# Attention beside a depthwise convolution: key blocks in batches of 7, 7, 7, 7 and 8, and other places for the small steps

## The chip, the cores and the metric

The kernel runs on one core of one Trainium2 chip. The metric is device time in microseconds (us) of one execution. The engines are TensorE (PE, its weight loads PEld), VectorE (DVE), ScalarE (ACT), GpSimd (POOL) and SyncE (SP); SP and POOL are used here mostly to issue DMA transfers.

## What is computed

```python
B, C, H, W = 4, 384, 48, 48          # N = 2304 tokens, 8 heads of 48
x_flat = x.reshape(B, C, N).transpose(0, 2, 1)
local = depthwise_conv_7x7(x) * bn_scale + bn_shift
local_q = layernorm(local_flat)                      # over channels
q, k, v = heads(layernorm(x_flat) @ qkv_w.T + qkv_b)
q = q + heads(local_q)
attn = softmax(q @ k.T * 48 ** -0.5)
out = x_flat + (attn @ v) @ proj_w.T + proj_b        # back to B, C, H, W
```

Everything is fp32.

## The kernel before

**Tiling.** Channels lie on the 128 partitions (three chunks), tokens along the free dimension. An image has NA = 5 groups of image rows for its queries (ROWS = 8, 10, 10, 10, 10, so 384 or 480 columns), 20 groups t = 5b + g in all. Keys and values are made per image in six parts of 384 tokens. Eight heads make four pairs; a pair's 2304 keys are 18 blocks of 128, so a group has 4 x 18 = 72 blocks.

**Order of the stages.** The first image's keys and values are made (0 to 152 us), then the loop over t at L1314 runs. Ahead of each later image's first group stands a key and value stage (L1316 to L1383), in which the output projection of the image before runs too. Then comes the loop over slots (L1389 to L1489), in which the group's attention runs.

**A slot.** A group has NSLOT = 12 slots, each a batch of BATCH = 6 blocks. `score_batch` (L1156) scores six blocks: `score` (L1126) is six matmuls (three passes, as queries and keys are split into a high and a low part of type fp32r, times two halves of the rows, one head each; L1133), and then ScalarE's exponential of the block (L1141) into a `pt` tile. `weigh_batch` (L1163) weighs them: `weigh` (L1144) is two fp32 matmuls of the 128 weights by the values and a column of ones (L1148; the trace shows four records a block), summed over the batch in one PSUM tile "o". `sums_out` copies the sums out on ScalarE: those of a pair's first batch into `ao` (or `aot` for the last pair, L1035), the others into a `part_o` tile (L1025), which VectorE adds later (`sums_add`, L1044). Scores and sums share the PSUM pool: four buffers of two banks, handed out in turn. There are four `pt` buffers and two of `part_o`.

**Keys.** A pair's high and low keys lie in DRAM (`wide`) and come in thirds of six blocks, 768 KB each, into one of three `ks` buffers (`load_keys`, L788, DMA at L791), most of them requested on POOL two slots ahead.

**Query parts.** `high_queries` (L992) writes the high part of a pair's queries on ScalarE (L996); `low_queries` (L998) the low part on VectorE (L1001), and sends both to other partitions by small DMAs on SP. The next pair's are made in the first slot of each pair: high after scoring, low after weighing. The last pair's queries are first gathered from the ends of the other three, by eight DMAs on SP (`gather_tails`, L721, into the tile `qt`). The last pair's outputs are sent back by six DMAs on SP at the end of `sums_add`.

**What runs beside it.** VectorE makes the next group's convolution, 49 taps for each of three chunks (`conv_ops`, L334; one instruction of L365 each, and the first tap on ScalarE by `first_taps`), from a slab of x that `load_slab` (L129) requests on POOL when the convolution of the group before begins. After it come the layer norm of the result (`Norm`, L567): a sum over chunks, a sum over partitions through DRAM (`out`, L661), `few_centre`, squares on ScalarE, again a sum, `few_root`, and its addition to the queries (`query_end`, L972). Groups t to 3 use a variant with means on TensorE (`early`). The next image's x is loaded in parts (`load_x`, L124) and normed in the same way. The output of the group before is divided by its denominators (`divide`, L1063) and held in DRAM (`hold`, L1096).

**Who sets the order.** The orders of TensorE, VectorE, ScalarE and SP are those in which the program is written; only POOL's is left to the framework's scheduler. A planner (`spare` L458, `plan` L528, `convolve` L542) deals the convolution's taps out over two points a slot, by guesses of VectorE's free time at each (`spare`) and by the point at which each group's convolution is due.

The functions that the change touches, and their callers:

Of the kernel before, what the change touches and what calls it, by code (L numbers as in the profile page):

```python
# [25 lines left out]
BATCH = 6  # L26
NSLOT = 12
X_SLOTS = 4, 7
X_LATER = 3
OUT_SLOT = 7  # L30
WARM = 14
SHIFTS = 4
AHEAD = 18
FIRST_ROOM = 4.0
# [14 lines left out]
def unshifted_pass(  # L49
# [119 lines left out]
    third = BATCH * P  # L169
# [164 lines left out]
    def conv_ops(t):  # L334
        b, g = divmod(t, NA)
        if 0 < t < NT - 1:
            load_slab(*divmod(t + 1, NA))
# [11 lines left out]
        for i, (tap, c) in enumerate(order):  # L349
            if i == len(order) - AHEAD and t + 1 < NT:  # L350
                if t:
                    begin_sums(t + 1)
                soon.append(lambda: first_taps(t + 1))
            part = window(slab, acc[:, c, :], g, first, end, c, tap)
            if not part:
                continue
            src, dst = part
            weight = cw[:, c, tap : tap + 1]
            if tap == taps[0]:
                if t == 0:  # L360
                    nc.vector.tensor_scalar(
                        dst, src, weight, shift[:, c : c + 1], ALU.mult, ALU.add
                    )
            else:
                nc.vector.scalar_tensor_tensor(dst, src, weight, dst, ALU.mult, ALU.add)  # L365
            if t == 0 or tap != taps[0]:
                yield
# [85 lines left out]
    def norm_slots(t):  # L453
        return (8 - (t > 0), None) if t + 1 < NA else (5, 8)

    def spare(t, s, half):
        b, g = divmod(t, NA)
        first, second = norm_slots(t)  # L458
        time = 3.6 - (0.0 if half else 0.6) - (0.6 if half and s % 3 == 1 else 0.0)
        if b + 1 < B and g >= begins(b + 1):  # L460
# [5 lines left out]
        if t + 1 < NA:  # L466
            if t:
                time -= {
                    (first, 0): 1.3,
                    (first + 1, 0): 1.4,  # L470
                    (first + 1, 1): 1.3,
                    (first + 2, 1): 4.3,
                    (first + 3, 1): 0.6,
                }.get((s, half), 0.0)
            else:
                time -= {(first + 1, 0): 1.4, (first + 2, 0): 4.3, (first + 2, 1): 0.6}.get(
                    (s, half), 0.0
                )
        elif g < NA - 1:
            time -= {  # L480
                (3, 1): 2.3, (5, 0): 1.2, (5, 1): 2.2, (6, 1): 2.3, (8, 0): 0.4, (8, 1): 1.5,
                (9, 0): 4.5,
            }.get((s, half), 0.0)
        return max(0.3, time) * columns_of(t) / G
# [21 lines left out]
    for t in range(NT):  # L506
# [3 lines left out]
        points += [("slot", t, s, h) for s in range(NSLOT) for h in range(2)]  # L510
        room += [spare(t, s, h) for s in range(NSLOT) for h in range(2)]
# [4 lines left out]
    for t in range(1, NT):  # L516
        last = ("slot", t - 1, norm_slots(t - 1)[0] - (t >= NA), t < NA) if t % NA else ("kv", t, 4, 0)
# [203 lines left out]
    def gather_tails(dst, src):  # L721

        for i, c in enumerate((*range(CC), 0)):
            for r in (0, 64):
                nc.sync.dma_start(
# [67 lines left out]
    def from_x(b, g, before=None, ao=None):  # L793
# [22 lines left out]
        def key(u, r):  # L816
# [7 lines left out]
            else:  # L824
                k = work.tile([P, 2, GM], HALF, tag="pt", name=f"k{b}_{g}_{u}", bufs=4)[:, :, :G]
# [146 lines left out]
    def query_end(t, at_once=False):  # L972
# [3 lines left out]
        q3 = work.tile([P, GM], F32, tag="qt", name=f"qt{t}", bufs=1)[:, : columns_of(t)]  # L976
        queries[t] = q, q3
# [36 lines left out]
    ended = []  # L1014
    parts_of = deque()

    def sums_out():

        if not ended:
            return  # L1020
        t, p, i, sums = ended.pop()
        n = columns_of(t)
        if i:
            part = work.tile([P, GM], F32, tag="part_o", name=f"o{t}_{p}_{i}")[:, :n]
            nc.scalar.copy(part[0 : 64 + HA], sums[0 : 64 + HA, 0, :n])  # L1025
            parts_of.append((t, p, i, part))
            return
        if p == 0:
            ao = work.tile([P, CC, GM], F32, tag="ao", name=f"ao{t}")[:, :, :n]
            ao3 = work.tile([P, GM], F32, tag="aot", name=f"aot{t}", bufs=1)[:, :n]  # L1030
            den = dram.tile([NH, n], F32, tag=f"den{n}", name=f"den{t}")
            outputs[t] = ao, ao3, den
        ao, ao3, den = outputs[t]
        dst = ao[:, p, :] if p < CC else ao3
        nc.scalar.copy(dst[0 : 64 + HA], sums[0 : 64 + HA, 0, :n])  # L1035

    def sums_add():
# [3 lines left out]
        t, p, i, part = parts_of.popleft()  # L1041
        ao, ao3, den = outputs[t]
        dst = (ao[:, p, :] if p < CC else ao3)[0 : 64 + HA]
        nc.vector.tensor_add(dst, dst, part[0 : 64 + HA])  # L1044
        if i < KB // BATCH - 1:
# [4 lines left out]
        if p == NP - 1:  # L1050
            for c in range(CC):
                for r in (0, 64):
                    nc.sync.dma_start(
# [69 lines left out]
    jobs, between = deque(), deque()  # L1123
    weighing = deque()

    def score(t, p, kb):  # L1126
        ks, qs = stacks[t // NA, p, kb // BATCH], stacked[t, p]
        at = slice(kb % BATCH * P, (kb % BATCH + 1) * P)
# [11 lines left out]
        pt = work.tile([P, 2, GM], F32, tag="pt", name="pt", bufs=4)[:, :, :n]  # L1140
# [3 lines left out]
    def weigh(i, sums):  # L1144
        t, p, kb, pt = weighing.popleft()
        for j in range(2):
            first = (kb % NB * NH + 2 * p + j) * HA
            nc.tensor.matmul(  # L1148
                sums[halves[j], 0, : columns_of(t)],
                lhsT=values[t // NA, kb // NB][:, first : first + 64],  # L1150
                rhs=pt[:, j, :],
                start=i == 0,
                stop=i == BATCH - 1,
            )

    def score_batch(t, s):  # L1156
        p, k0 = s // (KB // BATCH), s % (KB // BATCH) * BATCH
        for kb in range(k0, k0 + BATCH):
            score(t, p, kb)
            if between:  # L1160
                between.popleft()()

    def weigh_batch(t, s):  # L1163
        p, i = s // (KB // BATCH), s % (KB // BATCH)
# [4 lines left out]
        sums = two_banks("o")  # L1169
        for n in range(BATCH):  # L1170
            weigh(n, sums)
        ended.append((t, p, i, sums))
        sums_out()
# [139 lines left out]

    for t in range(NT):  # L1314
        b, g = divmod(t, NA)
        if g == 0 and b:  # L1316

            sums_add()
            load_x(b, NG - 1)
# [68 lines left out]
        first, second = norm_slots(t)  # L1388
        for s in range(NSLOT):  # L1389
            pair, part = divmod(s, KB // BATCH)  # L1390
            score_batch(t, s)
            if part == 0 and pair < NP - 1:
                high_queries(t, pair + 1)
            if s == 0:
                gather_tails(*reversed(queries[t]))
            if s == 0 and g == 0:
                keep_stack(b, 2)
            if (s or g) and (s < NSLOT - 2 or g < NA - 1):
                load_keys(b, s + 2, nc.scalar if g == 0 and s < 3 else nc.gpsimd)
            if s == 2 and g:  # L1400
                rb = divide(t - 1)
            if s == 0 and coming:
                load_x(b + 1, g - begins(b + 1))
            if s == NSLOT - 4 and g == NA - 1:
# [4 lines left out]
                else:  # L1409
                    places = [("acc", 3)] * 3 + [("sq", 2)] * 2 + [("qs", 5)]  # L1410
                    aos = []
                    for i in range(NG):
                        load_residual(b, i, *places[i])
                        aos.append(fetch(b, i) if i < NG - 1 else outputs[t][0])
            if coming and s == X_SLOTS[1] + 1:
                norm_x.scale(norm_x.few_newton())
            if following and s == second + 1:
                local_end(t + 1, norm.few_newton())
                query_end(t + 1, True)
            if coming and s == X_SLOTS[0] + 1:  # L1420
                jobs.extend(norm_x.square_jobs())
            if following and s == first + 1:
                jobs.extend(norm.square_jobs())
            if coming and s == X_SLOTS[1]:
                norm_x.few_variance()
            if following and s == second:
                norm.few_variance()
# [3 lines left out]
            else:  # L1431
                convolve("slot", t, s, 0)
            sums_add()
# [8 lines left out]
            if coming and s == X_SLOTS[1]:  # L1442
                norm_x.few_root()
            if following and s == second:
                norm.few_root()
# [3 lines left out]
            weigh_batch(t, s)  # L1449
            if early and s == first:  # L1450
# [5 lines left out]
            if early and s == first + (2 if t == 0 else 3):  # L1456
                low_queries(t + 1, 0, nc.gpsimd if t == 0 else nc.sync)
            convolve("slot", t, s, 1)
            if t and early and s == first + 2:
                local_end(t + 1, norm.newton())  # L1460
                query_end(t + 1)
            if part == 0 and pair < NP - 1:
                low_queries(t, pair + 1)
            if t and early and s == first + 1:
                norm.sum_squares()
            if following and s == second + 1:
                low_queries(t + 1, 0)
            if coming and s == X_SLOTS[0]:
                norm_x.few_centre()
            if following and s == first:  # L1470
                norm.few_centre()
            if s == OUT_SLOT and g:
                ao = outputs[t - 1][0]
                nc.vector.tensor_mul(ao, ao, rb)
                hold(t - 1)
            if coming and s == X_SLOTS[0] - 2:
                norm_x = Norm(xn[b + 1, g - begins(b + 1)])
                norm_x.sum()
                norm_x.out()
            if coming and s == X_SLOTS[0] + 1:  # L1480
                norm_x.sum_squares()
                norm_x.out()
# [566 lines left out]
```

## Time and profile before

| | |
|---|---|
| time, median of 4 runs | 2728.52 us (2726.93 to 2730.58) |
| the profiled execution | 2728.94 us, of which the span 2726.9 us |
| instructions | 46025 |
| attention of a ten-row group | 108.9 us |
| attention of an eight-row group | 88.5 us |
| key and value stage of images 1 to 3 | about 140 us each |
| the end (last projection and output) | 35 us |

The span runs from the first to the last instruction that the profile shows. TensorE's records carry modelled ends, since matmuls are pipelined: two that run in two halves of the array at once are booked at once, and a slower step between two matmuls is booked as busy. Register, branch, semaphore and DMA-issuing instructions count as no busy time, except that GpSimd's DMA issues are shown under POOL. The granted clock of TensorE is 1.0 in all stages but the last (0.99).

### The profile page before, as it was taken

To read this page: it belongs to the slowest core of one execution; us is meant where nothing else is said; L and a number is where in the kernel's file an instruction comes from. 1 tells how busy PE (TensorE), PEld (TensorE's weight loads), DVE (VectorE), ACT (ScalarE), POOL (GpSimd) and SP (SyncE) were. 2 spreads that over 40 slices of the span, in tenths; PEclk is the share of its full clock that TensorE was granted. 3 is DMA by queue.
4 is the path that set the end of the run, shared out by engine and by line. 5 is a ranking of instruction groups with operands and counts; after the bars stand their busy time and mean duration, and the time that the engine had idled before them with its cause. 6 is when DMAs were issued, how large, how long until landed. Compare 5 with 4: busy or idle time off the path is not lost.

```text
span 2726.9 us, 46025 instructions
## 1 busy us (share of the span) xinstructions
PE 2712.0 (99%) x16448; PEld 1533.2 (56%) x16448; DVE 2315.9 (85%) x4042; ACT 1671.2 (61%) x2318; POOL 591.1 (22%) x1055
## 2 busy tenths in 40 slices
PE   9999999999999999999999999999999999999999
PEld 6555555555556655555555655555555665555555
DVE  8999999989899999989889999889888888986212
ACT  4367767777325767676622777767752377776762
POOL 3531111102452111011155211111225501110110
PEclk9999999999999999999999999999999999999999
DMA  8454544546455545455455553545635544444442
GB/s 175 90 147 134 140 117 128 128 139 163 126 146 156 137 129 130 126 141 134 135 147 134 163 148 115 144 123 138 158 102 159 152 138 130 140 132 133 138 150 68
DMA packets 160209, 370.46 MB, mean 136 GB/s; under 512 B 58273, under 2 KB 107394, under 8 KB 159970
## 3 DMA queue, kind: packets, MB, share of 16 engines
q0 software_dynamic: 70496, 277.44, 35.4%
q1 hardware_dynamic: 84016, 79.92, 12.9%
q10 hardware_dynamic: 5458, 10.06, 1.2%
q8 instruction: 132, 2.16, 0.3%
q14 instruction: 107, 0.88, 0.1%
HBM read 258.14 MB, written 64.14 MB: 118 GB/s over the span
## 4 chain that ended last, share of the span: by engine, by line
PE 90%; DVE 5%; DMA 3%; ACT 0%; issue 0%; SPq 0%; POOL 0%; DVEq 0%; POOLq 0%; ACTq 0%
PE o L1148 41%; PE r L1133 34%; PE r L719 16%; DVE acc L365 4%; DMA xn<-in_x_dram 1%; DMA qs<-qs 0%; DMA staged<-in_qkv_wT_dram 0%; DVE k L829 0%; DMA slab<-in_x_dram 0%; DMA four<-parts 0%; PE r L618 0%; DMA wide<-k 0%; DMA out_dram<-xr 0%; DVE xn L714 0%; DMA parts<-part 0%
## 5 line engine op out<-in xcount | busy, mean ns | idle before, releaser
L365 DVE SCALAR_TENSOR_TENSOR acc<-slab,vec,acc 128x470 f32<-128x470 f32 (+10 forms) x2832 | 1657.7, 657 | 2.0 <-ACT acc L328 2.0
L1141 ACT ACTIVATE pt<-r 128x960 f32<-128x960 f32 (+1 forms) x1440 | 1248.5, 942 | 248.4 <-PE o L1148 153.0
L1148 PE MATMUL o<-pt,v 128*64 128x480 f32 (+1 forms) x5760 | 1166.2, 554 | 0.4 <-ACT pt L1141 0.4
L1133 PE MATMUL r<-qs,ks 64*128 64x480 f32 (+1 forms) x8640 | 966.8, 373 | 5.1 <-DMA qs<-qs 3.1
L1133 PEld LDWEIGHTS r<-qs,ks 64*128 64x128 f32 x8640 | 783.7, 184 | 269.7 <-issue 172.2
L1148 PEld LDWEIGHTS o<-pt,v 128*64 128x64 f32 x5760 | 392.5, 137 | 659.9 <-issue 566.2
L791 POOL DMA_DIRECT2D ks<-wide x220 | 160.1, 728 | 1362.8 <-PE r L1133 1285.6
L719 PE MATMUL r<-xn,w_qk 128*128 128x384 f32 x864 | 284.2, 486 | 0.0
L1025 ACT COPY o<-o 113x480 f32<-113x480 f32 (+1 forms) x160 | 87.1, 544 | 277.0 <-PE o L1148 276.4
L719 PEld LDWEIGHTS r<-xn,w_qk 128*128 128x128 f32 x864 | 164.0, 190 | 114.7 <-issue 0.7
L719 PE MATMUL r<-w_v,xn 128*128 128x384 f32 x432 | 145.3, 489 | 1.8 <-DVE xn L714 1.2
L813 ACT COPY v<-r 128x384 f32<-128x384 f32 x72 | 32.1, 480 | 185.0 <-PE r L719 185.0
L1044 DVE TENSOR_TENSOR ao<-ao,o 113x480 f32<-113x480 f32 (+1 forms) x120 | 75.9, 632 | 73.6 <-ACT o L1025 73.6
L719 PEld LDWEIGHTS r<-w_v,xn 128*128 128x128 f32 x432 | 81.2, 190 | 61.7 <-DVE xn L714 3.6
L776 POOL DMA_DIRECT2D wide<-k x144 | 72.3, 503 | 99.7 <-ACT k L826 79.4
L1001 DVE TENSOR_TENSOR qs<-xn,qs 128x480 fp32r<-128x480 f32 (+1 forms) x60 | 37.9, 632 | 62.1 <-ACT qs L996 62.1
L719 PE MATMUL r<-af,w_o 128*128 128x384 f32 (+1 forms) x270 | 85.2, 470 | 0.0
L1035 ACT COPY ao<-o 113x480 f32<-113x480 f32 (+1 forms) x60 | 32.7, 544 | 72.0 <-PE o L1148 72.0
L1044 DVE TENSOR_TENSOR aot<-aot,o 113x480 f32<-113x480 f32 (+1 forms) x40 | 25.3, 632 | 56.9 <-ACT o L1025 56.9
L843 ACT ACTIVATE xn<-r,qkb 128x384 f32<-128x384 f32 x72 | 39.7, 577 | 52.1 <-PE r L719 48.6
L1114 DVE SCALAR_TENSOR_TENSOR xr<-r,pb,xr 128x384 f32<-128x384 f32 (+2 forms) x72 | 42.0, 611 | 33.8 <-PE r L719 26.0
L719 PEld LDWEIGHTS r<-af,w_o 128*128 128x128 f32 x270 | 51.3, 190 | 31.9
(154 smaller groups left out, 1339.7 us busy)
## 6 DMA issues: line engine op xcount, KB each, us to landing
ks<-wide POOLq DMA_DIRECT2D x220, 768.0 KB, 4.9
qs<-qs SPq DMA_DIRECT2D x349, 60.0 KB
slab<-in_x_dram POOLq DMA_DIRECT2D x22, 432.0 KB, 7.9
wide<-k POOLq DMA_DIRECT2D x96, 96.0 KB, 2.2
wide<-ks POOLq DMA_DIRECT2D x12, 768.0 KB, 5.6
xr<-in_x_dram POOLq DMA_DIRECT2D x16, 576.0 KB, 5.3
rb<-rden SPq DMA_DIRECT2D x32, 270.0 KB
held<-ao POOLq DMA_DIRECT2D x12, 720.0 KB, 3.8
```

The lines of the kernel that those rows point to most:

```text
L365: nc.vector.scalar_tensor_tensor(dst, src, weight, dst, ALU.mult, ALU.add)
L719: nc.tensor.matmul(dst, lhsT=weights(c), rhs=src(c), start=c == 0, stop=c == CC - 1)
L776: nc.gpsimd.dma_start(out=last[16 * u : 16 * u + 16, 0], in_=k[r : r + 16, 0])
L791: queue.dma_start(out=place_keys(b, p, i), in_=wide[b, p][:, :, at])
L843: nc.scalar.activation(src[:, i, :], q[:, :G], AF.Identity, bias=qkb[:, 0, i : i + 1])
L1001: nc.vector.tensor_sub(qs[:, 1, :], query_of(t, p), qs[:, 0, :])
L1025: nc.scalar.copy(part[0 : 64 + HA], sums[0 : 64 + HA, 0, :n])
L1044: nc.vector.tensor_add(dst, dst, part[0 : 64 + HA])
L1114: nc.vector.scalar_tensor_tensor(xr[:, co, :], m, pb[:, co : co + 1], xr[:, co, :], ALU.add, ALU.add)
L1133: nc.tensor.matmul(r[:, j, :n], lhsT=ks[rows, w, at], rhs=qs[rows, m, :], start=i == 0, stop=i == 2,)
L1141: nc.scalar.activation(pt, r[:, :, :n], AF.Exp, scale=SCALE)
L1148: nc.tensor.matmul(sums[halves[j], 0, : columns_of(t)], lhsT=values[t // NA, kb // NB][:, first : first + 64], rhs=pt[:, j, :], start=i == ...
```

## The change

- **Batches.** Groups t from 4 on (`few_slots`, 16 of 20) have 10 slots with batches of 7, 7, 7, 7, 8, 7, 7, 7, 7 and 8 blocks; groups 0 to 3 keep 12 of 6. Batches 2 and 7 hold the end of one pair and the start of the next: `weigh_batch` makes two sums for them. `sums_out` and `sums_add` know first and last sums instead of batch numbers, and in those two slots `sums_add` is called once more.
- **Buffers.** `pt` has five buffers instead of four, `part_o` one instead of two; the last pair's output takes the `qt` tile, that of the gathered queries, instead of one of its own.
- **Keys.** Third i+3 is requested in the slot in which third i's last block is scored.
- **Queries.** High and low parts of the next pair are made in slots 0, 2 and 5 (of 12) or 0, 2 and 4 (of 10) instead of 0, 3 and 6. The high part of the next group's first pair is made behind the fifth score of slot 7, its low part at that slot's end; before, they were made in slots 9 (of 12).
- **Tails.** `gather_tails` and the six DMAs of the last pair's output go to POOL, in slot 1 or 2 (the latter ones stay on SP ahead of a key and value stage and at the end).
- **Places.** Two tables say in which slot and at which of its four points each norm step, the division, the multiplication and the loads stand. The steps of a 10-slot group lie in other slots than those of a 12-slot group.
- **Loads.** The next slab is requested after 40 taps of a convolution rather than at its start; the next image's x during the group before the one in which it is normed, in slot 6 or 8, rather than in slot 0 of that group.
- **Planner.** `spare` has new guesses for 10 slots, and the convolution is due one slot after `q_sum`, slot 3 of 10.

The core of the diff (left out: the guesses in `spare`, the closures that call each step where its table says, and the lines that they replace):

```diff
-BATCH = 6
-NSLOT = 12
+THIRD = 6
+PLACES_10 = {
+    "x_sum": (1, 3), "x_centre": (3, 1), "x_squares": (3, 1), "x_sum_squares": (3, 3),
+    "x_variance": (5, 1), "x_root": (5, 1), "x_scale": (5, 3),
+    "next_x": (6, 0), "divide": (1, 1), "tails": (1, 3), "multiply": (5, 1), "fetch": (7, 0),
+    "q_sum": (2, 3), "q_centre": (4, 1), "q_squares": (4, 1), "q_sum_squares": (4, 3),
+    "q_variance": (6, 1), "q_root": (6, 1), "q_end": (6, 3), "q_high": (6, 3), "q_low": (7, 3),
+}
+BATCHES = {12: [6] * 12, 10: [7, 7, 7, 7, 8] * 2}
+HIGHS = {12: (0, 2, 5), 10: (0, 2, 4)}
+SLAB_AT = 40
...
     def conv_ops(t):
         b, g = divmod(t, NA)
-        if 0 < t < NT - 1:
-            load_slab(*divmod(t + 1, NA))
...
+            if i == SLAB_AT and 0 < t < NT - 1:
+                load_slab(*divmod(t + 1, NA))
...
+    def few_slots(t):
+        return t + 1 >= NA
+
+    def n_slots(t):
+        return 10 if few_slots(t) else 12
+
+    def batch(t, s):
+        sizes = BATCHES[n_slots(t)]
+        return sum(sizes[:s]), sizes[s]
...
-    def gather_tails(dst, src):
-
+    def gather_tails(t):
+
+        src = queries[t][0]
+        dst = work.tile([P, GM], F32, tag="qt", name=f"qt{t}", bufs=1)[:, : columns_of(t)]
+        queries[t] = src, dst
         for i, c in enumerate((*range(CC), 0)):
             for r in (0, 64):
-                nc.sync.dma_start(
+                nc.gpsimd.dma_start(
                     out=dst[r + 16 * i : r + 16 * i + 16], in_=src[r + HD : r + 64, c, :]
                 )
...
+        if first:
+            dst = partial(t, p)
+        else:
+            dst = work.tile([P, GM], F32, tag="part_o", name=f"o{t}_{p}", bufs=1)[:, :n]
+            parts_of.append((t, p, last, dst))
+        nc.scalar.copy(dst[0 : 64 + HA], sums[0 : 64 + HA, :n])
...
+    def tails_out(queue=nc.gpsimd):
+        while tails_of:
+            ao, ao3 = tails_of.pop()
...
-        pt = work.tile([P, 2, GM], F32, tag="pt", name="pt", bufs=4)[:, :, :n]
+        pt = work.tile([P, 2, GM], F32, tag="pt", name="pt", bufs=5)[:, :, :n]
...
     def score_batch(t, s):
+        start, n = batch(t, s)
+        for i in range(n):
+            score(t, *divmod(start + i, KB))
             if between:
                 between.popleft()()
+            while i == 4 and in_gap:
+                in_gap.popleft()()
...
-        sums = two_banks("o")
-        for n in range(BATCH):
-            weigh(n, sums)
-        ended.append((t, p, i, sums))
-        sums_out()
+        while i < end:
+            p, first = divmod(i, KB)
+            many = min(KB - first, end - i)
+            sums = two_banks("o")[:, 0]
+            for k in range(many):
+                weigh(k == 0, k == many - 1, sums)
+            sums_out(t, p, first == 0, first + many == KB, sums)
+            i += many
...
+            if few_slots(t):
+                start, n = batch(t, s)
+                if t == NA - 1 and s == 0:
+                    load_keys(b, 2)
+                for i in range(start // THIRD, (start + n) // THIRD):
+                    if i + 3 < NP * 3 or g < NA - 1:
+                        load_keys(b, i + 3)
+            else:
+                if s or g:
+                    load_keys(b, s + 2, nc.scalar if g == 0 and s < 3 else nc.gpsimd)
```

## The prediction

> **What bounds the kernel now.** I read the busy shares first, then the chain of waits, then one batch on the time line. Busy time of each engine as a share of the span, and the chain of work that ended last:
>
> ```profile
> PE 2712.0 (99%) x16448; PEld 1533.2 (56%) x16448; DVE 2315.9 (85%) x4042; ACT 1671.2 (61%) x2318; POOL 591.1 (22%) x1055
> ...
> PE 90%; DVE 5%; DMA 3%; ACT 0%; issue 0%; SPq 0%; POOL 0%; DVEq 0%; POOLq 0%; ACTq 0%
> PE o L1148 41%; PE r L1133 34%; PE r L719 16%; DVE acc L365 4%; DMA xn<-in_x_dram 1%; DMA qs<-qs 0%; DMA staged<-in_qkv_wT_dram 0%; DVE k L829 0%; DMA slab<-in_x_dram 0%; DMA four<-parts 0%; PE r L618 0%; DMA wide<-k 0%; DMA out_dram<-xr 0%; DVE xn L714 0%; DMA parts<-part 0%
> ```
>
> TensorE is the bound: 2712.0 of 2726.9 us, and 75% of the chain is the attention's two matmul lines. Its granted clock is 1.0 throughout, so nothing is to be had from the clock. The stages, cut at the groups' edges (length, then busy time by engine; the two rows are the attention of images 1 and 2, five groups each):
>
> ```profile
> 834.20:1358.50 524.30, 524.30 (x3602) 294.22 (x3602) 483.09 (x842) 373.88 (x493) 75.90 (x122) 1.00 0.50 139
> ...
> 1498.00:2021.00 523.00, 523.00 (x3596) 293.87 (x3598) 465.94 (x813) 373.80 (x492) 76.71 (x123) 1.00 0.50 139
> ```
>
> In these stages TensorE has no gap at all. A change there gains only if TensorE's own work gets shorter, and loses whatever idle time it puts in. So I look into "busy" itself: one batch of a ten-row group in narrow windows (start, length, what ran; a row holds what touches its window):
>
> ```profile
> 1214.16 2.98 PE L1133 MATMUL r<-qs,ks 64*128 64x480 f32 x26
> 1216.98 0.37 PE L1133 MATMUL r<-qs,ks 64*128 64x480 f32 x2
> 1217.28 0.62 PE L1148 MATMUL o<-pt,v 128*64 128x480 f32 x2
> 1217.28 1.03 PE L1148 MATMUL o<-pt,v 128*64 128x480 f32 x4
> 1221.36 0.97 PE L1148 MATMUL o<-pt,v 128*64 128x480 f32 x4
> 1222.26 0.70 PE L1133 MATMUL r<-qs,ks 64*128 64x480 f32 x4
> ```
>
> Both kinds run in pairs (two row halves, or two column halves, at once). In the steady part a pair of scoring matmuls takes (2.98-0.37)/12 = 0.2175 us, three pairs (0.65) a block; a pair of weighing matmuls 0.97-0.57 = 0.40, two pairs (0.805 at the exact 0.4025) a block. At a switch the steps are longer: last scoring pair to first weighing pair 1217.28-1216.98 = 0.30 (+0.08), first weighing step 1.03-0.57 = 0.46 (+0.06), last weighing pair to first scoring pair 1222.26-(1221.36+0.40) = 0.50 (+0.10), the first scoring step 0.70-0.375 = 0.325 (+0.11). That is about **0.34 us a batch** booked as busy. Check: the batch lasts 9.07 us, and 18 x 0.2165 + 12 x 0.4025 leaves 0.343.
>
> **The batches.** 16 of the 20 groups (t from 4) go from 12 batches to 10. Blocks and matmuls stay the same, so 16 x 2 x 0.343 = **-11.0 us**. In the three eight-row groups the switch is the same size (0.34 of 7.38 a batch). A batch that crosses a pair adds a second sum but no switch: both of its sums are weighing matmuls in a row. Sums copied and added per group stay 12 and 8.
>
> Longer batches press on ScalarE and on the four PSUM buffers that scores and sums share. Its time line in the same batch (in brackets, idle before and releaser):
>
> ```profile
> 1213.31 0.56 ACT L1025 COPY o<-o 113x480 f32<-113x480 f32 x1 [1.54 <-PE o L1148]
> 1214.14 3.56 ACT L1141 ACTIVATE pt<-r 128x960 f32<-128x960 f32 x4 [0.28 <-PE r L1133]
> 1218.41 1.83 ACT L1141 ACTIVATE pt<-r 128x960 f32<-128x960 f32 x2 [0.71 <-PE o L1148]
> ```
>
> An exponential takes 0.89 us where scoring a block takes 0.65, so ScalarE falls behind in the scoring part. The batch began at 1213.19; the fourth exponential ends at 1217.70, 4.51 after it (4.5 to 4.6 over the batches that I read; I take 4.58 and 0.87 for each more). The fifth waits for the first weigh, because four pt buffers are full; the fifth pt buffer takes this wait away, which the longer batches need. Every allocation needs the buffer of four allocations earlier. So the sums of a batch of n wait for exponential n-3:
> - n=7: the fourth, 4.58 and 0.05 for the handover = 4.63; the first weigh would come at 4.09+0.65 = 4.74. Slack 0.11: nothing. In eight-row groups (block 0.53, exponential 0.73) slack is 0.02: nothing, barely.
> - n=8: the eighth score waits for the fourth exponential, 4.63 against its natural 7 x 0.65 = 4.55; the sums wait for the fifth, 4.58+0.87+0.05 = 5.50 against 4.74+0.65 = 5.39. So the batch loses 0.11 at most; as the fourth ends between 4.5 and 4.6, I take 0.09. Eight-row: 0.17 by the same sum. There are 32 such batches, 26 of ten rows and 6 of eight: 26 x 0.09 + 6 x 0.17 = **+3.3 us**. Bounds: 0 if the fourth exponential ends 0.1 sooner; 32 x (0.09+0.184) = 8.8 if each late buffer also lays open a weight load (the 184 ns of L1133's LDWEIGHTS row, which lies beside matmuls now).
>
> **Query parts and norm steps.** TensorE's one long attention stall is in t=0, where pair 2's low part comes by DMA too late:
>
> ```profile
> 201.55 0.76 PE L1133 MATMUL r<-qs,ks 64*128 64x384 f32 x5 [2.08 <-DMA qs<-qs]
> ```
>
> The high and low parts now go out a slot sooner, so this goes; but t=1's norm (centre on VectorE, squares on ScalarE, means on TensorE) ends in the same slot, and what it waits for is then late next. Between -2.1 and 0 I take **-0.4**, nearer to 0. In the other groups the lines of waits show TensorE waiting for nothing from norms or queries; VectorE has 41 us of idle time in image 1 (524.30-483.09) and 57 in image 2, which hides the moved steps. If a norm came late, its price is what a weighing phase waits, of the order of one squares step (under 2 us) in each of the 12 groups that prepare a next one, kept in the range through the third rival.
>
> Single part_o buffer and the crossing slots' extra copy: ScalarE can copy the next part only when VectorE has added the last, nine us earlier in steady order. A copy is 0.56 us; where first taps and squares crowd the same slot (two or three slots in the run) a late copy holds a PSUM buffer. Between 0 and 2 x 0.56 I take **+0.5**.
>
> **POOL and SP.** Eight gathers and six tails a group move from SP to POOL's queue: small issues there take 0.50 to 0.56 us (the wide<-k rows), 14 x 0.53 = 7.4 us a group, 119 in all, beside POOL's 22% busy: no engine time on the path. But key loads stand behind them:
>
> ```profile
> POOL ks L791 <- PE r L1133: 1285.6, 181, 12.0
> POOL slab L114 <- DVE acc L365: 113.2, 15, 12.7
> ...
> ks<-wide POOLq DMA_DIRECT2D x220, 768.0 KB, 4.9
> ```
>
> (columns: total wait, times, longest; for the load, median us to landing.) POOL sits 7.1 us on average waiting for scores before each key load, so a load goes out the moment its buffer is free. By the order of the changed program that leaves about two batches, 19.5 us, before the keys are needed (14.4 for one third, the eighth, with no tails near); landing takes 4.9 (longest 11.4). Minus 7.4 of tails, 12.1 remain: hidden, with 7.2 to spare. The slab request 40 taps (some 26 us) later finds its buffer freed and waits less on POOL; it lands in 7.9 and is needed 100 taps on: 0. The next image's x lands in 5.6, a group ahead: 0. Without cover each would cost its landing once.
>
> [...]
>
> **Sum.** Against the profiled execution, 2728.94 (span 2726.9 and 2.0 around it; 0.4 above the median 2728.52 of the four runs): 2728.94 - 11.0 + 3.3 - 0.4 + 0.5 = 2721.3; I say **2721.5**. 0.2% is 5.5 us, about what a measurement of this kernel can tell from no change; so faster means under 2723.1, slower over 2734.0.
>
> **Rivals.**
> 1. *ScalarE sets the batch* (0.19). The slack of the 7-batches is 0.11 and 0.02 us; one more small ScalarE step ahead of the exponentials, and each loses about 0.05: 128 x 0.05 = 6.4, giving about 2728; with the full 8.8 bound and less of this, 2723 to 2731. For it: exponentials at 0.89 against 0.65. Against it: the fifth pt buffer, and ScalarE 61% busy.
> 2. *Keys late on POOL* (0.12, the slower side). If the scheduler of POOL puts a waiting slab request and the tails ahead of a key load, a mean slab wait of 113.2/15 = 7.5 and 7.4 of tails leave 19.5-14.9 = 4.6 against a landing of 4.9: it decides from there. At the longest wait, 12.7, keys are 5.3 late. At 1.5 us in each of 16 groups it costs 24: about 2745. No gain is left from 0.5 us a group, slower from 0.8. Against it: later slab requests wait less.
> 3. *Smaller losses elsewhere*: norm or sums late, part of rival 1's band, same price, not counted again.
> 4. *The switch cost isn't per batch* (0.05): if the 0.34 us is the pair's or the sums' cost (12 sums a group stay), nothing is gained and the 8-batches lose: 2729 to 2732. Against it: the lengthened steps sit at the switches between kinds.
>
> **Numbers.** The forecast's own band, 2719 to 2724, has 0.54; a better case, 2715 to 2719, 0.10 (8-batches free, t=0's whole 2.1 gained: 2728.94-11.0-2.1 = 2715.8); rival 1 0.19, rival 2 0.12, rival 4 0.05. Faster: 0.10 + 0.45 + 0.02 = 0.57; slower: 0.12 + 0.01 = 0.13; within 0.2%: 0.30. The range 2716 to 2733 leaves out most of rival 2 and the last of the better case.
>
> **What would show it.** Right: ten-row groups of 108.9 - 2 x 0.343 + 2 x 0.09 = 108.4 us, and attention of 524.3 - 10 x 0.343 + 8 x 0.09 + 2 x 0.17 = 521.9 us in image 1; the same four switch steps, ten times a group; idle time of about 0.1 released by exponentials at the eighth score or the first weigh of the 8-batches alone. Wrong: waits of TensorE for ks by DMA (rival 2), for exponentials in 7-batches (rival 1), or scoring and weighing steps that are no longer in their steady part as before.

## The result and the profile after

The changed kernel takes 2732.24 us (median of 32 runs, 2727.49 to 2736.31), the kernel before in the same runs 2728.28: ratio 1.0012, 95% interval 1.0007 to 1.0017. It is not faster by 0.3% but slower by 0.1%. The profiled execution took 2732.38 us, its span 2730.2, 3.3 more than before. Busy shares and chain of the changed kernel:

```profile
PE 2710.6 (99%) x16448; PEld 1540.3 (56%) x16448; DVE 2314.0 (85%) x4042; ACT 1660.8 (61%) x2318; POOL 718.4 (26%) x1317
...
PE 87%; DVE 7%; DMA 4%; issue 1%; SPq 1%; ACT 1%; POOL 0%; DVEq 0%; ACTq 0%
```

TensorE's busy time fell by 1.4 us only, while the span grew: about 5 us more of it idle. On the chain, VectorE and the DMAs gained what TensorE lost (90 to 87%). POOL's extra 127 us are DMA issues; TensorE waits for no keys in this trace.

To see where, I took the starts of all scoring and weighing phases from the trace (a phase lasts from its first matmul to the next phase's first, so it holds the wait ahead of the next) and compared each with the median of its size:

| | before | after |
|---|---|---|
| 6 blocks, ten rows: score, weigh | 4.097, 4.981 | 4.097, 4.981 (t=1 to 3) |
| 7 blocks | | 4.750, 5.786 |
| 8 blocks | | 5.505, 6.591 |
| ten-row group without stalls | 108.9 | 108.46 |
| eight-row group without stalls | 88.54 | 88.30 |

The bookkeeping of the 3.3 us, by groups: 13 ten-row groups x -0.44 and 3 eight-row groups x -0.24 are **-6.4**; the wait at the start of t=4, which the forecast had left out, is gone, -1.3; t=0 is 2.8 longer (100.59 against 97.83); the start of t=5 waits 2.1; t=7 stalls 4.0 and t=8 1.7; the stretch behind the last matmul took 0.5 more (5.6 against 5.0), and the rest is -0.1. So the batches gave 6.4 of the 7.7 us that were forecast for them, and four stalls (t=0, t=5, t=7 and t=8) took back 10.6. Image 1's groups t=6, t=7 and t=9, as stages (length, then busy time by engine, granted clock, share of the DMA engines, GB/s):

```profile
925.30:1033.80 108.50, 108.50 (x724) 59.72 (x720) 104.93 (x173) 75.35 (x95) 21.30 (x36) 1.00 0.51 138
1033.80:1146.30 112.50, 110.58 (x722) 60.80 (x720) 100.64 (x174) 78.61 (x103) 20.59 (x35) 0.98 0.46 128
...
1256.50:1364.90 108.40, 108.40 (x722) 59.53 (x720) 95.19 (x172) 76.21 (x96) 25.16 (x46) 1.00 0.54 143
```

The first and the last have no gap and last 108.4 to 108.5; that of t=7 is 4 us longer, with a clock of 0.98. The stall in t=7, on TensorE's and then ScalarE's and VectorE's time line:

```profile
1076.33 2.22 PE L1179 MATMUL r<-qs,ks 64*128 64x480 f32 x18
1080.47 5.42 PE L1179 MATMUL r<-qs,ks 64*128 64x480 f32 x30 [1.92 <-ACT o L1076]
```

```profile
1071.67 1.83 ACT L1187 ACTIVATE pt<-r 128x960 f32<-128x960 f32 x2 [0.44 <-PE o L1194]
1078.62 1.35 ACT L623 ACTIVATE sq<-xn 128x384 f32<-128x384 f32 x3 [5.12 <-DVE xn L726]
1079.88 0.54 ACT L1076 COPY o<-o 113x480 f32<-113x480 f32 x1
1080.32 4.41 ACT L1187 ACTIVATE pt<-r 128x960 f32<-128x960 f32 x5
```

```profile
1048.03 3.72 DVE L377 SCALAR_TENSOR_TENSOR acc<-slab,vec,acc 128x460 f32<-128x460 f32 x6
1058.70 0.34 DVE L1116 RECIPROCAL rd<-rd 128x30 f32<-128x30 f32 x1 [6.95 <-DMA rd<-den]
...
1077.23 1.36 DVE L726 SCALAR_TENSOR_TENSOR xn<-sq,xn 128x1152 f32<-128x1152 f32 x1
```

Read from the bottom up. VectorE stood 6.95 us before the reciprocal, as the denominators had not landed. Behind it all its steps are late, so the centre of the next image's x (L726) ends at 1078.6. ScalarE had reached the squares of that x at 1073.5 and waited 5.12 us, in front of the sums' copy and the exponentials of the next batch. TensorE scored three blocks, had no free PSUM buffer, and stood. The squares now lie in the same slot as their centre; in the kernel before they followed up to a slot later. There, in t=7, the centre ended at 1077.9 and ScalarE came to the squares at 1084.0, without a wait:

```profile
1076.56 1.36 DVE L689 SCALAR_TENSOR_TENSOR xn<-sq,xn 128x1152 f32<-128x1152 f32 x1
```

```profile
1083.96 1.35 ACT L586 ACTIVATE sq<-xn 128x384 f32<-128x384 f32 x3
```

Over the groups from t=4 on, the time from the centre's end to the moment at which ScalarE reached its squares was 5 to 13 us in the kernel before, and -0.4 to 5.9 in the changed one, with -5.1, -3.8 and -1.2 for x in t=7, t=8 and t=12. Of the lateness 3.2 us are hidden (5.1 against 1.9 us of idle TensorE in t=7, 3.8 against 0.6 in t=8), so t=12 lost nothing. VectorE's waits for denominators, in total, times, longest (24.1, 10, 7.1 in the kernel before):

```profile
DVE rd L1116 <- DMA rd<-den: 78.4, 16, 7.6
```

In t=0 and at the start of t=5 it is another cause, a query's low part that lands late:

```profile
173.04 4.09 PE L1194 MATMUL o<-pt,v 128*64 128x384 f32 x24
179.19 0.41 PE L1179 MATMUL r<-qs,ks 64*128 64x384 f32 x1 [2.06 <-DMA qs<-qs]
180.65 5.08 PE L1179 MATMUL r<-qs,ks 64*128 64x384 f32 x35 [1.05 <-DMA qs<-qs]
```

SP had issued its transfers by 173.2 (before: by 174.0, and they were there in time). But from 167.2 on, POOL's queue holds the slab's request, which is new there, the gathers and a key load, and the DMA engines are full until 183 (a share of 0.99 to 1.14 from 176 on). That the slab's transfer makes the low part late is argued so far; numbers 2, 3 and 7 below put it to the test.

### The profile page after: what moved, and what is told of

It reads as the page before. It is cut to its first block, busy times and chain, and to the rows that moved or that the text cites. A ratio compares the mean times of both kernels' runs of the same rounds, so it can differ in the third digit from the quotient of the medians.

```text
span 2730.2 us, 46130 instructions
## 1 busy us (share of the span) xinstructions
PE 2710.6 (99%) x16448; PEld 1540.3 (56%) x16448; DVE 2314.0 (85%) x4042; ACT 1660.8 (61%) x2318; POOL 718.4 (26%) x1317
## 4 chain that ended last, share of the span: by engine, by line
PE 87%; DVE 7%; DMA 4%; issue 1%; SPq 1%; ACT 1%; POOL 0%; DVEq 0%; ACTq 0%
PE o L1194 39%; PE r L1179 32%; PE r L756 15%; DVE acc L377 5%; DMA four<-parts 1%; DMA xn<-in_x_dram 1%; DMA parts<-part 1%; DMA qs<-qs 1%; DMA rd<-den 0%; DMA staged<-in_qkv_wT_dram 0%; DVE k L869 0%; SPq L1047 0%; DMA wide<-k 0%; PE r L655 0%; DVE sq L628 0%
## 5 line engine op out<-in xcount | busy, mean ns | idle before, releaser
L831 POOL DMA_DIRECT2D ks<-wide x226 | 165.8, 734 | 943.5 <-PE r L1179 901.8
L765 POOL DMA_DIRECT2D qt<-xn x160 | 77.1, 492 | 58.4 <-DMA ao<-aot 19.2
L1099 POOL DMA_DIRECT2D ao<-aot x96 | 46.9, 494 | 136.3 <-DVE aot L1085 129.4
L1116 DVE RECIPROCAL rd<-rd 128x30 f32<-128x30 f32 (+1 forms) x20 | 6.6, 332 | 78.4 <-DMA rd<-den 78.4
L126 POOL DMA_DIRECT2D slab<-in_x_dram x72 | 40.2, 564 | 116.5 <-DVE acc L377 115.8
```

The lines of the kernel that those rows point to most:

```text
L126: queue.dma_start(out=dst[p0 : p0 + piece.shape[0]], in_=piece)
L765: nc.gpsimd.dma_start(out=dst[r + 16 * i : r + 16 * i + 16], in_=src[r + HD : r + 64, c, :])
L831: queue.dma_start(out=place_keys(b, p, i), in_=wide[b, p][:, :, at])
L1099: queue.dma_start(out=ao[r + HD : r + 64, c, :], in_=ao3[r + 16 * c : r + 16 * c + 16])
```

## The experiments

Times beside a run of the kernel before on the same chip (2728 to 2730 us); ratios to it. Each started from the changed kernel; "theory" and "rival" are what I then held. Stalls are read from the trace of one execution each.

**1. Squares of x a slot later.**

```diff
-"x_squares": (3, 1), "x_sum_squares": (3, 3), "x_variance": (5, 1), "x_root": (5, 1), "x_scale": (5, 3)
+"x_squares": (4, 1), "x_sum_squares": (4, 3), "x_variance": (6, 1), "x_root": (6, 1), "x_scale": (7, 0)
```

> The changed kernel with the squares of the next image's x, the second sum and the steps behind it one slot later; all else as changed. Theory (ScalarE stands in front of three squares whose centre VectorE has not made yet, and the exponentials queue behind them): the two stalls of 4.0 and 1.7 us in t=7 and t=8 go, 5.7 us less than the changed kernel: about 2726.5 us. Rival (VectorE is simply short of time in these groups, and the wait moves to the next step that ScalarE takes from it, the root or the cast of the query parts): 2730 to 2733 us, with the idle time of TensorE in the same groups some slots later.

Measured: 2751.81 us, ratio 1.0082 (1.0069 to 1.0095). Both were wrong on the time, though the rival had the wait move on. The stalls in slot 4 of t=7 and t=8 did go, so that cause holds. But slot 5 of t=8 and of t=13 now stalls 7.0 us each: there the query norm's squares wait for their own centre (5.7 us late), which lies behind the moved steps on VectorE. The key and value stage of image 1 is 4.6 us longer (TensorE waits for the last x to be scaled), t=4 loses 3.9, and t=0 1.1 more.

**2. Slab requested after 0 taps.**

```diff
-SLAB_AT = 40
+SLAB_AT = 0
```

> The changed kernel with the slab requested at the start of the convolution again (after 0 taps instead of 40). Theory (the slab's 432 KB share the DMA engines with the query's low parts in t=0 and at the start of t=5): the waits for qs by DMA there, 5.2 and 2.1 us, go, and the one at the start of t=4, 1.3 us, comes back: 6 us less than the changed kernel, about 2726 us. Rival (the gathers on POOL's queue make the low parts late, not the slab): within 1.5 us of 2732.

Measured: 2732.94 us, 1.0011 (1.0002 to 1.0019). The cause in t=0 and t=5 holds: t=0 takes 98.24 instead of 100.59, and the start of t=5 waits for nothing. Of t=0's 5.2 us of stalls at slots 2 and 3, 1.6 stay, and 1.3 come in later slots (0.6 of it a wait for keys). The 1.6 have another cause, the single part_o buffer: TensorE stands for a copy of sums, and that copy waited 4.0 us for VectorE's addition of the part before it.

```profile
180.41 2.21 PE L1179 MATMUL r<-qs,ks 64*128 64x384 f32 x18 [0.97 <-ACT o L1076]
```

```profile
179.88 0.48 ACT L1076 COPY o<-o 113x384 f32<-113x384 f32 x1 [4.03 <-DVE ao L1085]
```

The start of t=4 stayed free as well, and t=7's stall went, unforeseen: VectorE waits 2.8 us there for the denominators instead of 6.95, which fits the chain above. Of the 8.5 us that were gained in these places, 6.0 were lost in the key and value stage of image 1, 146.5 us against 140.5: VectorE waits 6.1 us there for a norm's round trip through DRAM, and TensorE then 3.2 for keys and 2.9 for an x. (The profiled execution took 2730.35 us; the median lies 2.6 above it, so the trace does not hold the whole time.) So the theory was right on its two places and wrong on the sum.

**3. Tails on SP's queue again.**

```diff
-                nc.gpsimd.dma_start(
+                nc.sync.dma_start(
...
-    def tails_out(queue=nc.gpsimd):
+    def tails_out(queue=nc.sync):
```

> The changed kernel with the eight gathers and the six sends of the tails back on SP's queue, at their new places. Theory (slab): nothing to be had, 2731 to 2734 us, the same waits for qs in t=0 and t=5. Rival (POOL's gathers): the wait of 5.2 us in t=0 goes, about 2727 us.

Measured: 2762.39 us, 1.0128 (1.0108 to 1.0148). Neither had foreseen it. In its trace SP issues in the order in which the program is written, and in the new places its norm transfers stand behind the gathers, 9.6 us behind the first of them in t=8:

```profile
1191.30 5.18 SPq L765 DMA_DIRECT2D qt<-xn  x8
...
1200.92 0.59 SPq L708 DMA_DIRECT2D parts<-part  x1
1208.99 0.58 SPq L709 DMA_DIRECT2D four<-parts  x1
```

```profile
1211.59 0.25 DVE L718 TENSOR_REDUCE few<-four 128x15 f32<-128x60 f32 x1 [14.16 <-DMA four<-parts]
```

VectorE had made these sums by 1197.4, where its wait for them begins (1211.59 - 14.16). They go out at 1200.9, behind the gathers, and only when they have landed, at 1209.0, may they be fetched; VectorE stands 14.2 us. So POOL's queue is worth about 30 us here (the runs lie between 2753.7 and 2775.9): I had called the move free, and it nearly is, but taking it back is not. In t=0, 3.8 of the 5.2 us of stalls stayed and the start of t=5 waited 2.5, so POOL's gathers are at most a part of the cause there.

**4. Everything but the batches.** Twelve slots of 6 in all groups, the norm steps of the groups from t=4 in their old slots; the keys are again requested slot by slot.

```diff
     def n_slots(t):
-        return 10 if few_slots(t) else 12
+        return 12
...
+PLACES_12_LATE = {
+    **PLACES_12,
+    "q_sum": (3, 3), "q_centre": (5, 3), "q_squares": (6, 0), "q_sum_squares": (6, 3),
+    "q_variance": (8, 0), "q_root": (8, 1), "q_end": (9, 0), "q_low": (9, 3),
+}
```

> All of the change but the batches: twelve batches of 6 in every group, with the norm steps of groups from 4 on in the slots that they had before, five pt buffers, one part_o buffer, tails on POOL, slab after 40 taps. Theory (ten batches save 6.4 us net, the squares' new places cost 5.7, the slab's request 5 to 7 in t=0 and t=5): 6.4 more and 5.7 less than the changed kernel, about 2733 us, ten-row groups of 108.9 us, no idle time in t=7 and t=8. Rival (the batches themselves are worth nothing or cost): 2726 to 2729 us.

Measured: 2733.21 us, 1.0013 (1.0004 to 1.0022). The theory had 2733; that it agrees to 0.2 us is chance, as the interval is 2.5 us to either side. Ten-row groups take 108.9 us, eight-row groups 88.5, and there is no stall in t=5 to t=19. Set beside the trace of the changed kernel: ten batches save 6.4 us, and their tables of places cost 5.7 in t=7 and t=8 and 2.1 at t=5, where the slab after 40 taps does no harm with twelve slots. What is nearly the same in both is t=0 (101.0 against 100.6); the key and value stage of image 1 is 2.6 longer here, and I did not trace why. The rival, that batches are worth nothing, is out.

**5 to 7. The reciprocal a slot later, with the slab after 40, 0 and 75 taps.** The denominators are still fetched in slot 1.

```diff
-"divide": (1, 1),
+"sums_in": (1, 1), "divide": (2, 1),
...
-SLAB_AT = 40
+SLAB_AT = 0      # number 6; 75 in number 7
```

> The changed kernel, but in 10-slot groups the denominators are only requested at the old point of the division (slot 1, ahead of the weighing) and VectorE takes their reciprocal a slot later (slot 2, same point). Theory (VectorE, which works in order, stands 4 to 7.6 us a group before the reciprocal, 78 us in all, and everything behind it, the centres of the norms too, is late by that; ScalarE's squares and then the exponentials wait for it): VectorE's wait for rd falls below 20 us in all, the stalls in t=7 and t=8 (4.0 and 1.7 us) go, about 2726.5 us. Rival (the planner gives VectorE too many taps there and the centre stays late): the stalls stay, 2731 to 2733 us.

> The same, and the slab requested at the start of the convolution. Theory: as with the later division, and t=0 another 2.4 us shorter, the start of t=5 another 2.1, if the key and value stage of image 1 loses its 6 us of waits too (they would then come from a late VectorE): about 2722 us. Rival (those 6 us come from small transfers that lie behind large ones, wherever the slab is requested): 2727 to 2729 us with the stage still at 145 to 147 us.

> The later division, and the slab requested after 75 taps instead of 40. Theory (slab and low parts collide in t=0 because the request falls into slots 1 to 3 there): the 5.2 us of t=0 and the 2.1 us at the start of t=5 go or shrink by the moved request, 2720 to 2724 us. Rival (any place of the slab collides with some small transfer of the query parts, since the DMA engines are busy all the time): 2726 to 2731 us, with waits for qs or for norms by DMA elsewhere.

Measured: 2736.02 (1.0025, 1.0015 to 1.0036), 2737.95 (1.0038, 1.0024 to 1.0051) and 2731.76 us (1.0013, 1.0004 to 1.0022). In number 5, VectorE's waits for denominators and for the norms' sums:

```profile
DVE few L718 <- DMA four<-parts: 55.8, 19, 9.6
...
DVE rd L1116 <- DMA rd<-den: 3.4, 2, 1.9
```

The 78.4 us went to 3.4, and the stalls in t=7 and t=8's slot 4 are gone: the theory's chain holds. But the time did not fall. VectorE now comes sooner to the norms' sums and waits there instead (35.6 to 55.8 us, longest 9.6), and the query's squares in slot 5 of t=8 and t=13 wait 5.5 and 5.0 us for their centre; TensorE loses 5.0 and 4.2 by it. In number 6 the key and value stage stays at 147.2, as the rival had it, though not "wherever the slab is requested": in number 7 it is 140.9. The time of number 6 met neither forecast. In number 7 the wait at the start of t=5 is gone, the stalls in t=8 and t=13 stay (3.3 and 5.6), and that in t=0 stays too (100.4), since POOL's queue, whose order the scheduler makes, still issues the slab at 168.2 (167.2 with 40 taps; at 124.0 with 0, in number 2). The rival of number 7 called the DMA engines busy all the time; in that trace their share is 1.03 from 170 to 180 and 0.62 from 180 to 185, and in the groups of image 1 in the changed kernel 0.46 to 0.54.

**8 to 10. Query norm a slot later.** Number 8 has the later reciprocal, number 9 also the slab after 0 taps in t=0 and after 75 elsewhere, number 10 that slab and the reciprocal where the change has it.

```diff
-"q_centre": (4, 1), "q_squares": (4, 1), "q_sum_squares": (4, 3), "q_variance": (6, 1), "q_root": (6, 1),
-"q_end": (6, 3), "q_high": (6, 3), "q_low": (7, 3)
+"q_centre": (4, 1), "q_squares": (5, 1), "q_sum_squares": (5, 3), "q_variance": (7, 1), "q_root": (7, 1),
+"q_end": (7, 3), "q_high": (7, 3), "q_low": (8, 3)
...
-            if i == SLAB_AT and 0 < t < NT - 1:
+            if i == (0 if t == 1 else SLAB_AT) and 0 < t < NT - 1:
```

> The kernel with the later division (two stalls of 5.0 and 4.2 us left, in t=8 and t=13), and in 10-slot groups the query norm's squares and all steps behind them one slot later. Theory (the centre comes up to 6 us late, since the norm's two transfers through DRAM take longer beside large loads, and ScalarE's squares stood only a few us behind it): with 10 us more both stalls go: 9.2 us less than the later division, about 2727 us; what is left over the sum of the batches are the 5 to 6 us of t=0 and 2 us at the start of t=5. Rival (the lateness moves on to the root, the cast or the low part, which are now nearer to the next group): 2731 to 2740 us, with waits of TensorE at the starts of groups.

> The same, and the slab requested at the start of the convolution in t=0 and after 75 taps of it in all other groups. Theory (each stall that I saw taken away): t=0 98.2 us, no stall at the start of t=5, key and value stages as before, groups of 108.45 and 88.3: about 2721.5 us, the prediction's number. Rival (large loads and small round trips share busy DMA engines, so each move brings another late transfer): 2724 to 2730 us.

> The same slab requests and the later query norm, but the division where the change has it. Theory (VectorE's 78 us of waiting for the denominators makes the centre of the next image's x late, in image 1 above all): 2 to 6 us more than with the later division, idle time in t=7 and t=8, 2723 to 2728 us. Rival (the division's place doesn't matter by itself): the same as the later division within 1 us.

Measured: 2742.75 (1.0057, 1.0044 to 1.0071), 2739.15 (1.0041, 1.0027 to 1.0054) and 2747.31 us (1.0076, 1.0063 to 1.0090). The rival was right in number 8 on the kind of wait, and its range ended just below: no squares of these steps wait for a centre any more, in any group, but the low part leaves in slot 8 and lands too late, so that the next group waits ahead of and in its first scores (8.4 us in t=11, 2.8 in t=6, 1.0 in t=7). In slot 9 of t=5 the single part_o buffer costs another 1.0: the copy waits 3.5 us for VectorE's addition. In number 9 both slab stalls went as expected (t=0 98.25, t=5's start free by the slab), but the waits at the groups' starts stayed, so that its time lies far above both forecasts. That large loads lengthen a norm's transfers through DRAM, as the theory of number 8 has it, was my estimate; the traces show VectorE's waits for them (in number 5 up to 9.6 us), not what a load adds. Number 10 is 8 us slower than number 9 (its forecast was 2 to 6 more): with the reciprocal early, x's squares stall t=7 (3.9), as in the changed kernel, and t=13 (2.1). So the place of the division matters by itself.

**11 and 12. Both slab places with the later reciprocal; and the query's squares half a slot later, the steps behind them packed.**

```diff
-"q_squares": (4, 1), "q_sum_squares": (4, 3), "q_variance": (6, 1), "q_root": (6, 1), "q_end": (6, 3), "q_high": (6, 3),
+"q_squares": (4, 3), "q_sum_squares": (5, 1), "q_variance": (6, 3), "q_root": (6, 3), "q_end": (7, 1), "q_high": (7, 2),
...
-                jobs.extend(norm.square_jobs())      # number 12 alone, as the table
+                in_gap.extend(norm.square_jobs())
...
```

> The later division, and the slab at the start of the convolution in t=0 and after 75 taps elsewhere; the query norm where the change has it. Theory (each stall has its own cause): the later division's 2736 us less 2.3 in t=0 and 2.1 at the start of t=5: about 2731.5 us; left over are t=8 and t=13 (4 to 5 us each, q's squares ahead of their centre). Rival (stalls move when any large transfer moves): some other wait of 2 us or more instead, 2733 us or more.

> The same, but the query norm's squares stand half a slot later, behind the fifth exponential of slot 5, and the steps behind them closer together, so that the low part still leaves at the end of slot 7. Theory (the chain from the due convolution to the low part is bound at both ends: squares too early wait for the centre, a low part too late makes the next group wait): neither stall is left, t=8 and t=13 lose 4 to 5 us each, about 2722 us, faster than before by 0.2%. Rival (the chain is too long for a ten-slot group wherever its slack is put): waits for the root or the cast appear in slots 7 and 8 or for qs at the group's start, 2728 us or more.

Measured: 2730.87 us (1.0006, 0.9997 to 1.0015) and 2728.57 us (0.9994, 0.9985 to 1.0003). Number 11 is as the theory had it to 0.6 us: stalls of 4.7 and 3.9 us in t=8 and t=13, t=0 98.2, t=5 free. Apart from the slab's place in the groups behind t=0 it is number 6, and the key and value stage of image 1 takes 141.0 us for 147.2: it was the request after 0 taps in a later group that cost it. In number 12 the stalls in t=8 and t=13 went as well, and it is the fastest: below the changed kernel, and no different from the kernel before that could be measured. Its forecast of 2722 failed by 6.6 us. Its groups from t=5 on are 5.3 us longer in all than 108.45 and 88.30 each, by small stalls at new places: 1.7 in slot 2 of t=11, 1.3 in slot 9 of t=5, and others of 0.2 to 0.6. That of t=5:

```profile
913.23 0.48 ACT L1076 COPY o<-o 113x384 f32<-113x384 f32 x1 [4.06 <-PE r L1179]
```

```profile
912.59 0.56 DVE L1085 TENSOR_TENSOR ao<-ao,o 113x384 f32<-113x384 f32 x1
```

The copy starts when VectorE's addition of the part before it ends (912.59 + 0.56 = 913.15): the single part_o buffer, with VectorE late. The line names a scoring matmul as the releaser, but the copy reads no scores; in number 8 the same copy's line names VectorE's addition. A version with two part_o buffers was not run.

## Why the prediction was wrong, point by point

The number was 2721.5, the measured time 2732.2. That lies inside the stated range of 2716 to 2733, but by luck: the bands of rivals 1 and 3 ended at 2731, rival 4's mechanism is out, and what filled the gap are stalls that the sum had at nothing.

- **The switches and the 8-batches: right in kind, a little too large.** The forecast was -11.0 and +3.3, so -7.7; measured -6.4 (number 4 and the table). A ten-row switch came out at 4.097 + 4.981 - 6 x (0.653 + 0.805) = 0.33 us for the forecast's 0.343, with a block's cost taken as the difference of 7 and 6 blocks; an eight-row switch by the same sum is 0.30. The check in the prediction took 0.2165 us a pair where its own line gave 0.2175; with that it leaves 0.325. The 8-batch's loss was 5.505 - (4.097 + 2 x 0.653) = 0.10 for a forecast of 0.09, and about 0.16 for 0.17 in eight-row groups. The 7-batches lose nothing, as forecast. The waits are where they were expected, at the eighth score and the first weigh, on the weight loads of the steady group t=9:

```profile
1298.93 4.42 PEld L1179 LDWEIGHTS r<-qs,ks 64*128 64x128 f32 x42 [0.76 <-issue]
1303.57 0.51 PEld L1179 LDWEIGHTS r<-qs,ks 64*128 64x128 f32 x6 [0.22 <-ACT pt L1187]
1304.44 0.20 PEld L1194 LDWEIGHTS o<-pt,v 128*64 128x64 f32 x4 [0.35 <-ACT pt L1187]
```

- **"In the other groups ... VectorE has 41 us of idle time in image 1 ... which hides the moved steps": the step that failed.** It took an image's idle time for slack at the place. A step in an in-order queue is covered only by the time between it and its user, and the new tables cut that from 5 to 13 us to -0.4 to 5.9, and to -1.2, -3.8 and -5.1 in three places, in a queue that now also stops for denominators (78 us instead of 24). Priced at 0, it cost 5.7, in t=7 and t=8. The third rival named it, but at under 2 us a group and inside the first rival's band; t=7 alone lost 4.0, part of it to a granted clock of 0.50 over 3.4 us, which the prediction had left out ("nothing is to be had from the clock").
- **"The slab request ... 0": failed.** I weighed when the slab is needed, not what it collides with. Together with the ten-slot places it costs 2.1 at the start of t=5 (number 4 has the same request and no wait there). In t=0 the old stall of 2.1 us did go, but new ones took the place of the gain: +2.8 where -0.4 stood. Numbers 2, 9 and 11 take the wait at t=5 and 2.3 of t=0's 2.8 away.
- **The reciprocal's new place** was in the change, and I did not weigh it. In t=7 of the kernel before, SP sent for the denominators at 1045.7 and VectorE took the reciprocal at 1053.4, after a wait of 3.5:

```profile
1053.40 0.34 DVE L1070 RECIPROCAL rd<-rd 128x30 f32<-128x30 f32 x1 [3.48 <-DMA rd<-den]
```

  In the changed kernel VectorE is there at 1051.75, SP sends for them at 1052.0, behind the low parts of a query, and the whole way of 6.7 us lies open.
- **Tails on POOL at nothing: right** in that no key load was late. That they can't stay on SP in these places (30 us, number 3), I had not seen.
- **The single part_o buffer** at +0.5: a bound that was too low. In t=0 of the changed kernel too the copy waits 4.0 us for VectorE's addition, but behind the late query, which hides it. With the slab moved (numbers 2, 6 and 9 to 12) it leaves 1.6 us in slot 3 of t=0, and in numbers 8 and 12 it costs 1.0 to 1.3 in slot 9 of t=5.
- **The rivals:** keys late on POOL did not happen in the changed kernel; the switch cost is per batch, as the groups without stalls show; ScalarE did set the batch in two groups, but through a wait of its own for VectorE, not through its load.

What stays open: 0.5 us behind the last matmul of the changed kernel, which I did not trace to a cause, and whether places exist that bring the 6.4 us home; number 12 loses 5.3 of them in other stalls.

## What to carry to other kernels

In hand-ordered queues, price a moved step by the time between it and the first waiter in line, at the slowest that the trace shows for what it waits on, not by the idle share of its engine. Moving a large transfer can move what collides with it, as the slab's did here (2.1 us at the start of t=5 after 40 taps; 147.2 against 141.0 us in the key and value stage after 0): look at which small round trips are under way at its new time. A gain of 0.4 us a group is used up by one stall of 4 us in ten groups.

## What I had not expected of the hardware

In t=7 a short stall of TensorE cost more than its idle time, 3.99 us for 1.92. The windows around it (granted clock third from the right):

```profile
1078.00:1080.00 2.00, 0.55 (x6) 0.15 (x2) 2.00 (x4) 1.38 (x4) 0.73 (x1) 1.00 0.94 274
1080.00:1082.00 2.00, 1.53 (x12) 0.97 (x12) 1.90 (x4) 2.00 (x3) 0.00 (x0) 1.00 1.05 357
1082.00:1084.00 2.00, 2.00 (x14) 1.53 (x12) 1.93 (x5) 2.00 (x4) 0.00 (x0) 0.50 0.50 180
1084.00:1086.00 2.00, 2.00 (x14) 1.46 (x12) 2.00 (x4) 0.73 (x1) 0.00 (x0) 0.65 0.04 3
1086.00:1088.00 2.00, 2.00 (x12) 0.70 (x12) 1.93 (x4) 1.05 (x2) 0.72 (x1) 1.00 0.29 49
```

TensorE idled 1.92 us, and about 1.5 us after it had resumed its granted clock was 0.50 for 3.4 us (1082.0 to 1085.4); the phase lost 3.99 in all; half of 3.4, so 1.7, is an estimate of the clock's part in it. In t=0 the same came after 2.06 and 1.05 (0.50 from 181 to 184); after the single waits of 1.32 (t=5) and 0.62 (t=8), and after the kernel before's 2.08 in t=0, the clock stayed at 1.00. In number 1, 4.5 idle became 7.0 lost, with 6.8 us at a clock of 0.50. Few matmuls ran around the stall in t=7: 14 began between 1078 and 1082, where 2 x 4/0.2175 = 37 would at the steady pace. The length of one gap does not decide by itself in these runs: 1.92 us in t=7 was followed by 0.50, and 2.08 in the kernel before was not. In the key and value stage of image 1 in number 2, TensorE waits 3.2 us and, 3.2 us of work later, 2.9, and the 18 matmuls behind that take 6.07 us, as they do behind the wait of 0.8 in the kernel before. What decides was not shown.
